# A routed feed-forward layer behind a graph convolution: loading and turning the first slot within the convolution, more row buffers, and slot tables in two steps

## The chip, the cores and the metric

The kernel runs on one core of a Trainium2 chip. A core has five engines that run their own instruction streams in order: TensorE (PE in the profile; its weight loads are listed apart as PEld), VectorE (DVE), ScalarE (ACT), GpSimd (POOL) and SyncE (SP, which here only issues DMAs; SPq in the profile is its DMA queue, POOLq that of GpSimd). Engines wait for each other and for DMAs on semaphores. On-chip memory is SBUF (128 partitions) and PSUM, in which TensorE accumulates. The metric is the device time of one execution in microseconds (us). The kernel before took 2367.03 us, the median of 15 runs (2361.11 to 2371.93).

## The reference

Four layers with residual connections over 3125 nodes of 256 features: a graph attention layer, a dense mixture layer, a graph convolution (GNN) and a routed feed-forward layer (FFN). The change lies in the last two. Cut to these:

```python
# graph convolution, 2 layers, on layer-normed x
x = relu(input @ weight + bias)
for i in range(2):
    h = x @ conv_w[i]
    msg = h[s] * (dinv[s] * dinv[d])[:, None]          # edges and self-loops
    x = relu(segment_sum(msg, d, num_segments=3125) + conv_b[i])
# x_total = x_before + x

# routed FFN on xt = layernorm(x_total)[3125, 256], 8 experts of width 1024
probs = softmax(xt @ Wr + br)
top_p, top_idx = top_k(probs, 2)
weights = top_p / top_p.sum(-1, keepdims=True)
xn = layernorm(xt)
xe = xn[None] * ln_g[:, None] + ln_b[:, None]          # of each expert
h = gelu(einsum('end,edh->enh', xe, W1) + b1)
y = einsum('enh,ehd->end', h, W2) + b2
out = x_total + sum over the two chosen experts of weights * y[expert]
```

## The kernel before

**The build.** The program is written with tiles taken from pools. A pool with n buffers of a name makes the n+1st tile wait until all users of the first are done. The build adds the waits and orders the instructions of each engine itself; within an engine the order is then fixed. So "is issued after" below is the order of the code, and an engine may run a few instructions in another order.

**The second convolution.** The nodes are 25 blocks of 128. `layer(1, ...)` in `graph_convolutions_fast` goes over five groups of `GB` = 5 blocks (b0 = 0, 5, 10, 15, 20). For each group it loads the counts of edges between blocks in five pieces (`cnt_h`, three buffers, by SP), casts each piece (`cnt_r`, two buffers: three fifths on ACT at L1093, two fifths on DVE at L1094), and adds 125 matmuls of 128x128 by 128x512 into five PSUM accumulators `po` (L1099). When a block is summed, DVE scales both halves of `po` (L1112, L1114) and adds to the residual stream (L1173). After the last block of a group, the tasks of `Router.tasks` for this group go into a list `spare`; `layer` calls these between the matmuls of the next group. The tasks of the last group (b0 = 20) are called in the routed slots.

**Routing.** For one group of blocks: layer norm into `rt_xt` (L1030); five `logits` (a block is turned on PE into PSUM `aux` and multiplied with `wr`, L2479); `choose` (softmax and the two best, DVE and ACT); four empty tasks; `place` (two matmuls with a strict lower triangle and with ones count how many rows each expert has had before; DVE makes the row index and the marks weight and node number); a second layer norm; five `send`. A `send` makes two rows per node of 258 numbers, the 256 features copied by ACT (L2551) and the two marks by DVE (L2552), in a tile `rt_row` that has four buffers, and scatters each of the two to the DRAM array `rows` by an indirect DMA of POOL (L2553). `rows` has a range for each expert. Then five `begin` store the blocks of the residual stream to `out` (L2563), to which the slots later add.

**Slots.** The routed layer is computed in slots of 256 rows of one expert (24 full ones, then half ones). Slots 0 to 7 (`SOON` = 8) take rows of blocks below 15 (`KNOWN`) alone, since after group b0 = 10 it is known how many slots those fill. `close(15)`, after the sends of group b0 = 10, makes the table of the expert and first row of these slots (`share_soon`), and `close(25)`, after the sends of the last group, that of all others (`share_late`). Both end with twelve small matmuls against `close_mine` that put each slot's bias and layer norm vectors into columns (L2600 and L2607 in the profile; there as 16 and 8, since each of these float32 matmuls has two records) and two ACT copies. `add_up` (L2630) makes running sums of 8 or 16 columns by as many additions, each of one column to the one before.

For a slot s, `load(s)` reads expert and first row from the table into SP's registers and issues on SP the rows `xr` (L2708, 264 KB), the weights w1 and w2 (L2715 and L2717, 1 MB each) and the bias b2 (L2719). The load of rows waits for the scatters that may hold its rows: for slots below 8 those of blocks below 15, for later ones all. Because they are in one DRAM array, the build also makes any scatter and any load wait for what stands before it, unless they are declared to have nothing to do with each other; the scatters are so among each other (`apart(ins, "rows")`). `front(s)` turns the rows with four PE transposes into PSUM (L2732, tile `tr`), scales them by the slot's vectors into `xe` (DVE, L2735), and makes the output indices `free` (L2741) and `to` (L2743) from the marks. `slot(s)` computes eight pieces `ph` of the hidden layer (L2757) with GELU on ACT (L2759), calls `front` of the next slot, then two `py` (L2767), adds bias and weight on DVE into `y` (L2770, L2771) and adds the rows to `out` by an indirect DMA of POOL (L2772). A full slot has 32 records of ph and 32 of py. After each piece of ph and of py one task is taken from `spare` as long as there are any.

**Where slot 0 stands.** `load(0)` is called after `layer(1, ...)`, from the pool `ahead`. `begin_slots` then calls `load(1)` and `front(0)`, and in a loop over s = 0 to 7 `load(s + 2)` and `slot(s)`. At s = 6 the tasks still in `spare` are called at once, since `load(8)` needs the late table.

Of the kernel before, what the change touches and what calls it, by code (L numbers as in the profile page):

```python
# [11 lines left out]
F32 = mybir.dt.float32  # L12
# [749 lines left out]
class Fast(Kernel):  # L762
# [277 lines left out]
    def graph_convolutions_fast(self, I, router, experts, out):  # L1040
# [5 lines left out]
        with ExitStack() as ctx:  # L1046
# [129 lines left out]
                    spare.extend(router.tasks(b - GB + 1, GB, out))  # L1176
            layer(1, work, finish1)

            router.load(0, I)
            second.close()  # L1180
            router.begin_slots(out, I)

# [1177 lines left out]
class Router:  # L2360
# [15 lines left out]
    def __init__(self, k):  # L2376
        self.k, self.tc, self.nc = k, k.tc, k.nc
        NS, SLOT = self.NS, self.SLOT
        self.rows = k.dram.tile([8 * self.RANGE + SLOT, self.W], F32, name="rows")
        self.scatters, self.spare, self.at = [], deque(), {}  # L2380

    def prepare(self, ctx):
        nc = self.nc
        NS, NF = self.NS, self.NF
        pool = self.pool = ctx.enter_context(self.tc.tile_pool(name="router", bufs=1, reuse_waits="tile"))
        self.more = pool.tile([1, 1], I32, name="more")

        self.parts = [(0, self.SOON), (self.SOON, NS - self.SOON)]
# [32 lines left out]

    def open(self, ctx, aux, I):
        nc = self.nc
        work = ctx.enter_context(self.tc.tile_pool(name="route_work", bufs=1, reuse_waits="tile"))
        self.ahead = ctx.enter_context(self.tc.tile_pool(name="ffn1_ahead", bufs=1, reuse_waits="tile"))
        self.work, self.aux = work, aux
# [29 lines left out]
    def tasks(self, b0, n, out):  # L2456
# [89 lines left out]
        def send(i):  # L2546
            b = b0 + i
            m = min(P, N - b * P)
            for r in range(2):
                row = work.tile([P, self.W], F32, name="rt_row", bufs=4)  # L2550
                nc.scalar.copy(row[:, :D], st["xt"][:, i, :])  # L2551
                nc.vector.tensor_copy(row[:, D:], st["mark"][:, r, i, :])  # L2552
                ins = nc.gpsimd.indirect_dma_start(  # L2553
                    out=self.rows, out_offset=bass.IndirectOffsetOnAxis(
                        ap=st["index"][:m, r, i:i + 1], axis=0),
                    in_=row[:m, :], in_offset=None)
                self.apart(ins, "rows")
                self.scatters.append((b, ins))

        def begin(i):  # L2560
# [3 lines left out]
            if b0 + n == NB:  # L2564
                self.tc.declare_no_dep(ins.ins, group="soon",
                                       reason="the first slots' rows are of earlier blocks")

        each = range(n)
        tasks = ([norm] + [lambda i=i: logits(i) for i in each] + [choose] +
                 [lambda: None] * 4 + [place, renorm] + [lambda i=i: send(i) for i in each])  # L2570
        if b0 + n in (self.KNOWN, NB):
            tasks.append(lambda: self.close(b0 + n))
        return tasks + [lambda i=i: begin(i) for i in each]

    def close(self, blocks):


        nc = self.nc
        late = blocks == NB
        n = self.parts[late][1]  # L2580
        table, b1, ln = self.table[late], self.b1[late], self.ln[late]
        one = lambda shape, name: self.work.tile(shape, F32, name="close_" + name, bufs=1)
        total = one([P, 8], "total")
        nc.vector.tensor_sub(total, self.next[:, blocks, :], self.next[:, 0, :])
# [6 lines left out]
                                op0=ALU.min)  # L2591
        nc.vector.tensor_scalar(owner, owner, 7.0, None, op0=ALU.min)
        nc.vector.tensor_copy(table[:, 0, :], owner[0:1, :])
        mine = one([8, n], f"mine{n}")
        nc.vector.tensor_scalar(mine, owner[:8, :], self.part[:8, :], None, op0=ALU.is_equal)
        rows, F = self.rows8, self.F
        ps = self.pl.tile([P, 512], F32, name="pl")[:, :self.NF * n].rearrange(
            "p (c s) -> p c s", s=n)
# [24 lines left out]
        nc.vector.tensor_reduce(begin, past, AX.X, ALU.add)  # L2623
        nc.vector.tensor_sub(begin, unit, begin)

    def add_up(self, first, need, m):
        nc = self.nc
        nc.vector.memset(first[:, 0:1], 0.0)
        for e in range(m):
            nc.vector.tensor_add(first[:, e + 1:e + 2], first[:, e:e + 1], need[:, e:e + 1])  # L2630

    def share_soon(self, n, total, owner, begin, one):

        nc, SLOT, J = self.nc, self.SLOT, self.SOON
# [7 lines left out]
        self.add_up(first, need, 8)  # L2642
        slot = one([P, n], "slot")
        nc.gpsimd.iota(slot, pattern=[[1, n]], base=0, channel_multiplier=0,
                       allow_small_or_imprecise_dtypes=True)
        self.owners(n, 8, first, slot, need, owner, begin, one)
        nc.vector.tensor_scalar(begin, begin, float(SLOT), None, op0=ALU.mult)
        nc.vector.tensor_scalar(first, first, float(n), None, op0=ALU.min)
        nc.vector.tensor_sub(self.done, first[:, 1:], first[:, :8])

    def share_late(self, n, total, owner, begin, one):
# [20 lines left out]
        self.add_up(first, units, 16)  # L2672
        nc.vector.tensor_add(units, units, at[:, :16])
        nc.vector.tensor_sub(units, units, at[:, 1:])

# [18 lines left out]
    def load(self, s, I):  # L2694
# [12 lines left out]
        xr = pool.tile([P, 2, self.W], F32, name="xr")[:, :self.blocks(s)]  # L2707
        load = nc.sync.dma_start(xr, self.rows[ds(at, self.blocks(s) * P), :].rearrange(  # L2708
            "(i p) w -> p i w", p=P))
        if s < self.SURE:  # L2710
            for b, scatter in self.scatters:
                if late or b < self.KNOWN:
# [9 lines left out]
    def front(self, s):  # L2722
# [1 line left out]
        nc, work = self.nc, self.slot_work  # L2724
        late = s >= self.SOON
        i = s - self.parts[late][0]
        ln, m = self.ln[late], self.blocks(s)
        xr, w1, w2, b2 = self.at.pop(s)
        pt = self.ps_t.tile([P, 2, 2, P], F32, name="tr")
        for c in range(2):  # L2730
            for h in range(m):
                nc.tensor.transpose(pt[:, c, h, :], xr[:, h, c:D:2], self.k.ident)  # L2732
# [3 lines left out]
                                    ln[:, 0, c, i:i + 1], ln[:, 1, c, i:i + 1], op0=ALU.mult,  # L2736
                                    op1=ALU.add)

        to = work.tile([P, 2], I32, name="to", bufs=6)[:, :m]
        free = work.tile([P, 2], F32, name="free", bufs=2)[:, :m]  # L2740
        nc.vector.tensor_scalar(free, xr[:, :, D + 1], 0.0, float(2 * NP), op0=ALU.is_lt,  # L2741
                                op1=ALU.mult)
        nc.vector.tensor_add(to, free, xr[:, :, D + 1])  # L2743
# [37 lines left out]
    def begin_slots(self, out, I):  # L2781
# [5 lines left out]
        with tc.tile_pool(name="ps_h0", bufs=2, space=PSUM, reuse_waits="tile") as self.ps_h, \  # L2787
                tc.tile_pool(name="ps_t0", bufs=1, space=PSUM, reuse_waits="tile") as self.ps_t, \
                tc.tile_pool(name="ps_y0", bufs=2, space=PSUM, reuse_waits="tile") as self.ps_y:
            self.load(1, I)  # L2790
            self.front(0)
            for s in range(self.SOON):
                if s + 2 == self.SOON:
                    while self.spare:
                        self.spare.popleft()()
                self.load(s + 2, I)
                self.slot(s, s + 1, I, out)

# [92 lines left out]
```

## Time and profile before

One execution was profiled; all times below of parts of the kernel are of this one.

| what | value |
|---|---|
| median of 15 runs | 2367.03 us (2361.11 to 2371.93) |
| profiled execution, own time | 2364.63 us |
| its span on the core | 2362.8 us |
| mean granted TensorE clock | 0.945 of full speed |
| PE busy | 2053.6 us (87%) |
| PEld busy | 1712.1 us (72%) |
| DVE busy | 1335.0 us (57%) |
| ACT busy | 1085.7 us (46%) |
| POOL busy | 808.7 us (34%) |

The busy time in 40 slices of 59 us each shows where the engines are full; each digit is a tenth of the slice:

```
PE   5577788888988876899999699979989978999996
DVE  7798576768777763278888443334327664212221
ACT  3498556555666546044544254434434433222231
POOL 1777777777777723000000500000001313221221
PEclk9999999999999888999999799989999988999998
DMA  7545575756767759962221100033325445667773
```

The stretch of this change lies in slices 31 to 34 (counted from 1): the second convolution with its routing from 1750 on, the end of the convolution at 1929.98, slot 0 from 1943.71 and slot 1 from 1963.71. From there on the slots follow each other to the end. PEclk is the clock granted to TensorE in tenths; it is 8 where the others around it are 9. The busy time of a group of instructions in the profile holds its work at a low clock too, so a longer busy time may be the same work. An idle time in the profile is followed by what ended it: "9.07 <-DMA xr<-rows" means that PE stood still for 9.07 us and that the load of xr from rows ended it.

### The profile page before, as it was taken

The page shows a single profiled execution, that of the slowest core. Times are in us where ns is not written, and L with a number is a line of the kernel's source. Part 1 is how long each engine was busy: PE and PEld are TensorE (multiplying, and loading weights), DVE is VectorE, ACT ScalarE, POOL GpSimd, SP SyncE. Part 2 cuts the span into 40 slices and gives each one's busy share as a digit, 9 for nine tenths or more (in the row PEclk, how much of TensorE's full clock was granted, in tenths as well). Part 3 has the DMA queues.
Part 4 walks back from the last instruction along what each step waited for, and adds up shares of the span by engine and source line. Part 5 has one row for each costly group of instructions (what it writes and reads, how often), then busy time and mean ns, then how long its engine had stood idle before and what let it go on. Part 6 is the DMA issues. An engine that isn't in the chain of part 4 may idle for free. (4 is left out here: it accounts for less than half of the span.)

```text
span 2362.8 us, 35957 instructions
## 1 busy us (share of the span) xinstructions
PE 2053.6 (87%) x10512; PEld 1712.1 (72%) x10512; DVE 1335.0 (57%) x4399; ACT 1085.7 (46%) x2496; POOL 808.7 (34%) x801
## 2 busy tenths in 40 slices
PE   5577788888988876899999699979989978999996
PEld 5356677666766655788887588858877767888886
DVE  7798576768777763278888443334327664212221
ACT  3498556555666546044544254434434433222231
POOL 1777777777777723000000500000001313221221
PEclk9999999999999888999999799989999988999998
DMA  7545575756767759962221100033325445667773
GB/s 233 154 122 153 133 209 141 211 168 195 200 190 212 204 159 324 319 209 82 73 70 47 40 1 1 1 111 113 124 100 169 150 135 181 189 190 226 215 215 72
DMA packets 236521, 356.91 MB, mean 151 GB/s; under 512 B 37356, under 2 KB 177923, under 8 KB 232603
## 3 DMA queue, kind: packets, MB, share of 16 engines
q1 hardware_dynamic: 194315, 258.97, 33.9%
q0 software_dynamic: 39008, 92.91, 15.4%
q10 hardware_dynamic: 2992, 2.62, 0.4%
q8 instruction: 88, 1.44, 0.3%
q14 instruction: 118, 0.97, 0.1%
HBM read 268.69 MB, written 86.20 MB: 150 GB/s over the span
## 5 line engine op out<-in xcount | busy, mean ns | idle before, releaser
L1876 POOL DMA_INDIRECT edge_rows<-table,pick x566 | 591.4, 1045 | 184.0 <-issue 74.3
L1961 PE MATMUL edge_sums<-edge_moves,edge_rows 128*128 128x120 f32 x2264 | 332.3, 294 | 76.0 <-DVE agg L1974 74.7
L1961 PEld LDWEIGHTS edge_sums<-edge_moves,edge_rows 128*128 128x128 f32 x2264 | 309.0, 206 | 113.7 <-DVE agg L1974 91.6
L1099 PE MATMUL po<-parts,cnt_r 128*128 128x512 f32 x1250 | 311.0, 404 | 14.6 <-ACT cnt_r L1093 9.4
L1099 PEld LDWEIGHTS po<-parts,cnt_r 128*128 128x128 f32 x1250 | 236.5, 192 | 64.6 <-ACT cnt_r L1093 10.2
L854 PE MATMUL po<-h,w 128*128 128x257 f32 x1250 | 277.0, 382 | 3.5 <-ACT o L1006 2.3
L854 PEld LDWEIGHTS po<-h,w 128*128 128x128 f32 x1250 | 237.2, 191 | 39.0 <-ACT o L1006 3.9
L1764 PE MATMUL ps<-hot_key,hot_lo 128*128 128x350 f16 (+2 forms) x782 | 193.1, 335 | 70.5 <-DVE acc L1790 35.0
L1782 ACT CAST acc<-ps 128x325 f32 (+2 forms) x391 | 179.1, 458 | 140.2 <-PE ps L1764 106.5
L1744 DVE TENSOR_SCALAR hot_key<-iota_key,key 128x350 f16<-128x350 f16 (+2 forms) x782 | 235.4, 330 | 4.4 <-PE ps L1764 3.2
L2759 ACT ACTIVATE hid<-ph,ffn_b 128x256 f32<-128x256 f32 (+1 forms) x232 | 105.8, 456 | 263.5 <-PE ph L2757 261.0
L2757 PE MATMUL ph<-xe,ffn_w 128*128 128x256 f32 (+1 forms) x928 | 194.4, 367 | 3.6 <-DVE rt_xt L1030 3.6
L2772 POOL DMA_INDIRECT out<-y,to x53 | 82.6, 1559 | 317.1 <-DVE y L2771 171.7
L2767 PE MATMUL py<-ffn_w,hid 128*128 128x256 f32 x848 | 189.8, 381 | 1.3 <-ACT hid L2759 1.3
L2757 PEld LDWEIGHTS ph<-xe,ffn_w 128*128 128x128 f32 x928 | 165.1, 194 | 27.0 <-DVE rt_xt L1030 3.9
L2767 PEld LDWEIGHTS py<-ffn_w,hid 128*128 128x128 f32 x848 | 159.3, 191 | 22.0 <-ACT hid L2759 1.7
L839 ACT ACTIVATE z<-z,att_cols 128x640 f32<-128x640 f32 x125 | 103.0, 828 | 146.2 <-DVE z L837 119.9
L1750 ACT ACTIVATE hot_lo<-iota_key,lo 128x128 f16<-128x128 f16 x494 | 170.0, 395 | 0.0
L1764 PEld LDWEIGHTS <-hot_lo 128*128 128x128 f16 x782 | 72.6, 104 | 117.1 <-ACT hot_lo L1757 42.6
L1093 ACT CAST cnt_r<-cnt_h 128x1920 fp32r<-128x1920 f16 x50 | 89.9, 1799 | 112.1 <-PE po L1099 102.9
L2433 POOL IOTA earlier<- 128x128 f32 x1 | 0.2, 243 | 395.0 <-PE po L1099 395.0
L845 DVE TENSOR_TENSOR w<-z,cnt 128x640 f32<-128x640 f32 x125 | 102.4, 820 | 41.3 <-PE po L854 38.4
(422 smaller groups left out, 3253.0 us busy)
## 6 DMA issues: line engine op xcount, KB each, us to landing
ffn_w<-in_L_ffn_W SPq DMA_DIRECT2D x58, 1024.0 KB
cnt_h<-cnt SPq DMA_DIRECT2D x50, 800.0 KB
rows<-blank SPq DMA_DIRECT2D x109, 258.0 KB
cnt<-acc SPq DMA_DIRECT2D x50, 400.0 KB
cnt<-cnt SPq DMA_DIRECT2D x25, 800.0 KB
normed<-first_out SPq DMA_DIRECT2D x20, 640.0 KB
first_out<-first SPq DMA_DIRECT2D x56, 192.0 KB
edge_rows<-table,pick POOLq DMA_INDIRECT x566
```

The costliest lines, as they stand in the source:

```text
L839: nc.scalar.activation(z, z, AF.Exp, bias=cols[:, 0, j:j + 1], scale=-1.0)
L854: nc.tensor.matmul(pos[i][:, :D + 1], lhsT=w[:, ts(i, P)], rhs=moving[:, j, :D + 1], start=(j == 0), stop=(j == NB - 1))
L1099: nc.tensor.matmul(pos[b], lhsT=c[:, j - j0, ts(b, P)], rhs=parts[i][:, j].rearrange("p a m -> p (a m)"), start=(j == 0), stop=(j == NB - 1))
L1744: nc.vector.tensor_scalar(h[:, u, :NB * w], self.wide[:, :NB * w], self.key[:, t:t + 1], None, op0=ALU.is_equal)
L1750: nc.scalar.activation(l[:, u, :], self.wide[:, :P], AF.Abs, bias=self.lo[:, t:t + 1], scale=-1.0)
L1764: last = self.nc.tensor.matmul(ps[:, :n], lhsT=l[:, u, :], rhs=h[:, u, :n], start=(u == 0), stop=(u == CT - 1))
L1782: ins = self.nc.scalar.copy(self.acc[g][:, :, ds(o + 1, width(c) - 1)], self.parts[c][:, :, 1:])
L1876: return self.nc.gpsimd.indirect_dma_start(out=self.ring[:, e % (RB * BT), :], out_offset=None, in_=self.table, in_offset=bass.IndirectOff ...
L1961: nc.tensor.matmul(ps[:, f * 4 * w:f * 4 * w + EW], lhsT=self.rows_of(m)[:, e, ts(f, P)], rhs=self.spread[m % 3][:, e * 5 * w:e * 5 * w + EW],
L2757: nc.tensor.matmul(ph, lhsT=w1[:, c, ts(f, P)], rhs=xe[:, c, :], start=(c == 0), stop=(c == 1))
L2759: nc.scalar.activation(hid[:, f, :], ph, AF.Gelu, bias=b1[:, f:f + 1])
L2767: nc.tensor.matmul(py, lhsT=hid[:, f, ts(i, P)], rhs=w2[:, f, :], start=(f == 0), stop=(f == NF - 1))
```

## The change

- `load(0)` is taken out from behind `layer(1, ...)`. The tasks of group b0 = 10 get it, at the end: `close(0)`, two empty tasks, `close_vectors(0)`, `load(0)`, then the five stores `begin`. That makes 28 tasks in this group instead of 24.
- `front(0)` is taken out of `begin_slots`. In the tasks of group b0 = 15 it takes the place of the third of the four empty tasks behind `choose`. It uses the PSUM tile `aux` instead of `tr`, and xe, to and free come from the pool `ahead` with one buffer.
- The row loads of slots 1 to 7 join the group of the scatters (`apart`): the build then makes none of them wait for a later scatter and no scatter wait for them. Their written dependency on the scatters of blocks below 15 stays. The load of slot 0 is not in the group.
- `rt_row` gets eight buffers instead of four.
- `close` is split in two: the tables, up to `close_mine`, and `close_vectors`, the twelve small matmuls and two copies. The late `close_vectors(1)` is called in slot 6, behind six empty tasks.
- `add_up` makes the running sums by doubling: three steps for 8 columns and four for 16, each a copy of the first columns and one addition of the others, in a new tile for each step but the last.

```diff
@@ graph_convolutions_fast
             layer(1, work, finish1)
 
-            router.load(0, I)
             second.close()
             router.begin_slots(out, I)
@@ Router.tasks, send
-                row = work.tile([P, self.W], F32, name="rt_row", bufs=4)
+                row = work.tile([P, self.W], F32, name="rt_row", bufs=8)
@@ Router.tasks
         each = range(n)
+        wait = lambda: None
+        first = (lambda: self.front(0)) if b0 == self.KNOWN else wait
         tasks = ([norm] + [lambda i=i: logits(i) for i in each] + [choose] +
-                 [lambda: None] * 4 + [place, renorm] + [lambda i=i: send(i) for i in each])
-        if b0 + n in (self.KNOWN, NB):
-            tasks.append(lambda: self.close(b0 + n))
+                 [wait, wait, first, wait] + [place, renorm] + [lambda i=i: send(i) for i in each])
+        if b0 + n == self.KNOWN:
+            tasks += [lambda: self.close(0), wait, wait, lambda: self.close_vectors(0),
+                      lambda: self.load(0, self.I)]
+        elif b0 + n == NB:
+            tasks.append(lambda: self.close(1))
         return tasks + [lambda i=i: begin(i) for i in each]
@@ Router.close
-        mine = one([8, n], f"mine{n}")
+        mine = self.mine[late] = one([8, n], f"mine{n}")
         nc.vector.tensor_scalar(mine, owner[:8, :], self.part[:8, :], None, op0=ALU.is_equal)
+
+    def close_vectors(self, late):
+
+        nc, n, mine = self.nc, self.parts[late][1], self.mine[late]
+        b1, ln = self.b1[late], self.ln[late]
         rows, F = self.rows8, self.F
...
@@ Router.add_up
-    def add_up(self, first, need, m):
-        nc = self.nc
+    def add_up(self, first, need, m, one):
+
+        nc, step = self.nc, 1
         nc.vector.memset(first[:, 0:1], 0.0)
-        for e in range(m):
-            nc.vector.tensor_add(first[:, e + 1:e + 2], first[:, e:e + 1], need[:, e:e + 1])
+        while step < m:
+            out = first[:, 1:] if 2 * step >= m else one([P, m], f"sums{m}_{step}")
+            nc.vector.tensor_copy(out[:, :step], need[:, :step])
+            nc.vector.tensor_add(out[:, step:], need[:, step:], need[:, :m - step])
+            need, step = out, 2 * step
@@ Router.load
+        if 0 < s < self.SOON:
+            self.apart(load, "rows")
         if s < self.SURE:
             for b, scatter in self.scatters:
                 if late or b < self.KNOWN:
@@ Router.front
-        ln, m = self.ln[late], self.blocks(s)
+        ln, m, deep = self.ln[late], self.blocks(s), 1 if s == 0 else 6
         xr, w1, w2, b2 = self.at.pop(s)
-        pt = self.ps_t.tile([P, 2, 2, P], F32, name="tr")
+        if s == 0:
+            work, pt = self.ahead, self.aux.tile([P, 512], F32, name="aux").rearrange(
+                "p (c h n) -> p c h n", c=2, h=2)
+        else:
+            pt = self.ps_t.tile([P, 2, 2, P], F32, name="tr")
...
-        to = work.tile([P, 2], I32, name="to", bufs=6)[:, :m]
-        free = work.tile([P, 2], F32, name="free", bufs=2)[:, :m]
+        to = work.tile([P, 2], I32, name="to", bufs=deep)[:, :m]
+        free = work.tile([P, 2], F32, name="free", bufs=min(deep, 2))[:, :m]
@@ Router.begin_slots
             self.load(1, I)
-            self.front(0)
             for s in range(self.SOON):
                 if s + 2 == self.SOON:
                     while self.spare:
                         self.spare.popleft()()
+                    self.spare.extend([lambda: None] * 6 + [lambda: self.close_vectors(1)])
                 self.load(s + 2, I)
                 self.slot(s, s + 1, I, out)
```

More of the change, by code (lines that the diff above doesn't have):

```diff
@@ L2379, in __init__ @@
         self.rows = k.dram.tile([8 * self.RANGE + SLOT, self.W], F32, name="rows")
-        self.scatters, self.spare, self.at = [], deque(), {}
+        self.scatters, self.spare, self.at, self.mine = [], deque(), {}, {}
     def prepare(self, ctx):
@@ L2386, in prepare @@
         self.more = pool.tile([1, 1], I32, name="more")
+        self.slot_work = None
         self.parts = [(0, self.SOON), (self.SOON, NS - self.SOON)]
@@ L2423, in open @@
         nc = self.nc
+        self.I = I
         work = ctx.enter_context(self.tc.tile_pool(name="route_work", bufs=1, reuse_waits="tile"))
@@ L2568, in tasks, with close @@
         each = range(n)
+        wait = lambda: None
+        first = (lambda: self.front(0)) if b0 == self.KNOWN else wait
         tasks = ([norm] + [lambda i=i: logits(i) for i in each] + [choose] +
-                 [lambda: None] * 4 + [place, renorm] + [lambda i=i: send(i) for i in each])
-        if b0 + n in (self.KNOWN, NB):
-            tasks.append(lambda: self.close(b0 + n))
+                 [wait, wait, first, wait] + [place, renorm] + [lambda i=i: send(i) for i in each])
[4 more added lines that the diff above has]
+            tasks.append(lambda: self.close(1))
         return tasks + [lambda i=i: begin(i) for i in each]
-    def close(self, blocks):
+    def close(self, late):
         nc = self.nc
-        late = blocks == NB
+        blocks = NB if late else self.KNOWN
         n = self.parts[late][1]
-        table, b1, ln = self.table[late], self.b1[late], self.ln[late]
+        table = self.table[late]
         one = lambda shape, name: self.work.tile(shape, F32, name="close_" + name, bufs=1)
@@ L2641, in share_soon @@
         first = one([P, 9], "first")
-        self.add_up(first, need, 8)
+        self.add_up(first, need, 8, one)
         slot = one([P, n], "slot")
@@ L2671, in share_late @@
         first = one([P, 17], "first_unit")
-        self.add_up(first, units, 16)
+        self.add_up(first, units, 16, one)
         nc.vector.tensor_add(units, units, at[:, :16])
```

## The prediction

> **What bounds the kernel now.** I read the engine table first: TensorE (PE) is busy 87% of a span of 2362.8 us, and nearly full in the last sixth. The change touches only the stretch from about 1800 to 2010 us: the second convolution's five groups, then the first three routed slots. There I read the waits of PE, then the busy time by stretch, then the lines around each gap.
>
> Waits of PE between 1800 and 2010 us (total, times, longest):
>
> ```profile
> engine line waited for: us in total, times, longest us
> PE tr L2732 <- DMA xr<-rows: 9.1, 1, 9.1
> PE pl L2600 <- DVE close_mine L2595: 5.4, 1, 5.4
> PE po L1099 <- DVE o L1114: 4.8, 2, 2.6
> PE ph L2757 <- DVE rt_xt L1030: 3.6, 1, 3.6
> PE pl L2600 <- issue: 2.2, 1, 2.2
> PE py L2767 <- ACT hid L2759: 1.3, 1, 1.3
> PE po L1099 <- DVE cnt_r L1094: 0.4, 1, 0.4
> ```
>
> These are 26.8 us of idle PE. The cost does not end with them: after most gaps the granted clock is about half. Busy time by stretch (PE, weight loads, DVE, ACT, POOL, then clock, DMA share, GB/s):
>
> ```profile
> 1885.00:1895.00 10.00, 10.00 (x32) 8.11 (x33) 3.51 (x11) 3.13 (x7) 5.46 (x6) 0.54 0.53 168
> 1944.00:1949.00 5.00, 5.00 (x15) 3.98 (x15) 2.67 (x13) 1.65 (x4) 0.00 (x0) 0.51 0.98 317
> 1949.00:1964.00 15.00, 15.00 (x86) 13.40 (x85) 7.88 (x29) 10.40 (x19) 0.25 (x1) 1.00 1.06 376
> 1985.00:1997.00 12.00, 12.00 (x40) 10.14 (x41) 1.11 (x4) 1.51 (x4) 4.50 (x3) 0.51 0.31 59
> 2012.00:2340.00 328.00, 328.00 (x1635) 290.59 (x1634) 67.23 (x190) 91.58 (x202) 70.67 (x46) 1.00 0.68 197
> ```
>
> PE is "full" at 0.51 to 0.54, doing half the work. Following the granted clock finely, the half-clock stretches are 1853.33 to 1856.74 (3.41), 1884.05 to 1894.29 (10.24), 1935.25 to 1948.90 and 1983.03 to 1996.69 (13.65 each). A stretch costs half of the part of it in which PE works. From 2012 on PE never waits, so what is saved before slot 2 is saved at the end.
>
> Where the gaps come from, from the timeline (start, length, instruction, idle before it and its releaser):
>
> ```profile
> 1853.25 8.00 PE L1099 MATMUL po<-parts,cnt_r 128*128 128x512 f32 x27 [2.61 <-DVE o L1114]
> 1932.86 0.96 POOL L2553 DMA_INDIRECT rows<-rt_row,rt_index  x1 [0.30 <-issue]
> 1936.10 0.41 SPq L2708 DMA_DIRECT2D xr<-rows  x1
> 1939.05 1.10 PE L2732 MATMUL tr<-ident,xr 128*128 128x128 f32 x4 [9.07 <-DMA xr<-rows]
> 1943.71 3.75 PE L2757 MATMUL ph<-xe,ffn_w 128*128 128x256 f32 x8 [3.56 <-DVE rt_xt L1030]
> 1984.92 3.58 PE L2600 MATMUL pl<-close_mine,rows 8*128 8x24 f32 x16 [5.39 <-DVE close_mine L2595]
> ```
>
> The reader should see a chain: the last of group 15's ten scatters starts at 1932.86; SP issues slot 0's row load 3.2 us later, when that has landed; the rows land at 1939.05; PE waits 9.07 us. And what DVE and ACT wait for in the same window:
>
> ```profile
> DVE rt_row L2552 <- DMA rows<-rt_row,rt_index: 30.2, 23, 3.8
> ACT rt_row L2551 <- DMA rows<-rt_row,rt_index: 36.9, 20, 5.0
> ```
>
> With four row buffers, the fifth to tenth row of each group wait for a scatter on an in-order engine, ahead of the sums that would free PE's accumulators.
>
> **The change part by part.** Times are on the axis of the profiled execution: span 2362.8, own time 2364.6, which is 2.4 under the median of the runs.
>
> *Eight row buffers.* A scatter lands 2.8 to 3.9 us after it starts, and POOL starts one per 1.27. Before, DVE is held until the sixth has landed (3.9 + 5 x 1.27 = 10.2 us from the first start), now until the second (5.2). It comes free 5 us earlier, more than either gap behind "o" (2.14 and 2.61, at 1814 and 1850). Both go, and with them the half-clock stretch behind the second (3.41 / 2 = 1.7): 6.4. Late next are the casts: four more row copies stand ahead of one on ACT, some 1.4 us by the row copies' 0.41 and the overlap of their starts, against some 1.75 of slack by my reading of the two orders. A bound from below is 4 (one stretch and one gap stay).
>
> *Slot tables of group 10.* PE's 2.22 gap before the small matmuls is a wait for the DVE chain. In the changed order these matmuls stand two convolution matmuls earlier (22 of the last 30 ahead instead of 24), and the chain is still behind the ninth row's wait. So I leave 2.0 of the gap. Whether the 10.24 of half clock recurs I can't read: 0 to 5.1 gained. I take half, 2.6: the gap before is unchanged in kind, but less idle time precedes it. Slot 0's four transposes move into the layer at 0.64 (full clock, from slot 1's row). Sum 0.2 + 2.6 - 0.6 = 2.2, ends -0.4 to 4.7.
>
> *Slot 0 loaded and turned early.* Its row load needs only blocks below 15, whose last scatter started at 1894.08, so it can land near 1900. Group 15's scatters (from 1921.48) now wait for it, with 21 us to spare. On SP the load (rows, 2 x 1 MB of weights, bias) goes ahead of five output stores and the 25th count load, which also waits for the lane of the first weight load. That count load is needed near 1915 and should be there by 1905: nothing. On DVE the "free" operation on slot 0's rows stands ahead of a cast; by my reading of the order it has 1.6 to 3.3 us of slack: nothing, but every us beyond is a us of PE. The first bias operations, xe (1.0 us on DVE) in group 15, lie beside PE.
>
> From the layer's end (1929.98) to slot 1's first matmul (1963.71) it took 33.7: 13.7 of waits and transposes, then slot 0's 20.0. Now slot 0's ph starts at once. The 20.0 holds 5.2 at half clock, 2.6 lost: 17.4 without. New is a wait in the middle: PE reaches slot 1's transposes after 12 ph matmuls (0.28 each, four took 1.11 at 1950.18: 3.3), but slot 1's row load is behind the stores of blocks 20 to 23 on SP, and these wait for DVE's last sums. On DVE five blocks take 1.12 each after the tenth row; the stores take 1.08 each to issue (two took 2.17 on SP). That puts the load some 4.3 after the layer's end, and rows land 2.95 after issue (1936.10 to 1939.05): 7.2, a wait of 3.9 and some 0.2 of restart, 4.1. It is long enough for a half-clock stretch; I take two of the short ones, 2 x 1.7 = 3.4, between 0 and 6.8. New: 17.4 + 4.1 + 3.4 = 24.9. Gain 8.8, ends 5.4 (stretch as long as the one now) and 12.2 (none).
>
> *Vectors of the late slots to slot 6.* From slot 1's first ph (1963.71) to slot 2's transposes (2001.44): 37.7. Steady slots take 14.3. Out go the 5.39 gap, the vector matmuls 3.58 + 1.90 = 5.5 at half clock, and half clock over the rest of that stretch (11.8 busy, less 5.5, by half: 3.1). 37.7 - 5.4 - 5.5 - 3.1 = 23.7; ACT's 1.30 gap stays; with 0.5 for place's matmul group, no longer behind a wait, 23.2. The 24 small matmuls come back in slot 6, 2.7 at full clock, 5.5 at half; I take 3.3. Gain 14.5 - 3.3 = 11.2, ends 5.8 (the 5.39 comes back as a wait of slot 2 for DVE) and 12.
>
> *Doubling.* 8 serial additions become 6 operations, 16 become 8. By the row "close_first_unit" six took 1.12 us, 0.19 each: 0.4 and 1.5 us less on DVE, with the copies off the chain. No PE work waits there any more except the small matmuls of group 10: nothing by itself.
>
> *Early loads free of later scatters.* Loads 1 to 7 lose a wait that only load 0 (30.4 us on SP's queue) showed large. Already priced above.
>
> Sum: 6.4 + 2.2 + 8.8 + 11.2 = 28.6. Profiled 2364.6 - 28.6 = 2336; against the median, 2338.
>
> [...]
>
> **The rivals.**
> 1. *Clock stays low at every gap that is left.* For it: gaps of 2.2 and 2.6 were each followed by it. Against: the gap of 2.14 at 1814 was not. Then 2.6 (tables) + 3.4 (slot 1's wait) + 2.2 (slot 6) less gain: 2338 + 8 = 2346.
> 2. *New waits take the place of the old.* Slot 2's xe, in DVE's order, stands behind the late tables' chain, and slot 1's rows come later still. Gives back 5.4 and, with a longer store queue, 4 and a further stretch of 5: 2338 + 14 = 2352. For it: DVE showed 30.2 us of row waits. Against: four more buffers remove most.
> 3. *Short gaps cost no clock.* 2.6 + 3.4 + 0.6 more: 2331.
> 4. *Slower.* Load 0 holds SP's queue: it waits for every scatter lane, and the 25th count load stands behind its weights. PE then starves in group 20. To lose 28.6 and 4.7 more, the count load would have to land 33 us after it is needed, near 1948 instead of 1905, or slot 0's rows be 35 us late at DVE. Scatters of group 10 all started by 1894.08, which speaks against it.
> 5. *It doesn't do what it says.* Load 0 lands late enough that slot 0 has to wait as before, and only the buffers gain: 2367 - 6 = 2361.
>
> **How the numbers follow.** Forecast 0.47, rival 1 0.22, rival 2 0.12, rival 3 0.09, rival 5 0.04, slower 0.06. Low: rival 3's 2331 less the upper ends of the buffers and slot 6, about 4: 2327. High: rival 2 with 2, 2354; above lie rivals 4 and 5. A measurement here tells 0.2% (4.7 us) from no change: faster 0.91, same 0.03, slower 0.06.
>
> **What would show it.** The wait of "tr" for xr falls from 9.1 to about 4 and names slot 1; "pl <- close_mine" 5.4 is gone, the 2.2 stays; "po <- o" 4.8 is gone; DVE's row waits fall from 23 times to about 8; clock near 1.00 through slots 1 and 2; PE continuous from about 1957 on. Wrong if PE shows waits for cnt_r in the last group (load 0 in the way), if slot 2's ph waits for xe, or if slot 6 shows a new gap.

## The result and the profile after

The changed kernel takes 2336.78 us, the median of six runs (2334.06 to 2340.68); the kernel before took 2366.96 in the runs beside it (31 runs). The ratio is 0.9876, 95% interval 0.9863 to 0.9890, so it is faster by 1.24%, 30 us. The forecast was 2338. The profiled execution took 2332.42, its span 2330.6.

The waits of PE between 1800 and 2010 us of the changed kernel (total, times, longest):

```profile
PE pl L2611 <- issue: 2.0, 1, 2.0
PE tr L2753 <- DMA xr<-rows: 1.5, 1, 1.5
PE ph L2778 <- DVE o L1114: 0.9, 1, 0.9
PE aux L1037 <- DVE rt_xt L1030: 0.6, 1, 0.6
```

Five us of waits stand where there were 26.8. The 9.1 for slot 0's rows, the 3.6 behind it, the 5.4 for "close_mine" and both gaps behind "o" are gone; the 2.2 ahead of the early small matmuls is still there as 2.0. New are 1.5 for slot 1's rows, 0.9 for the last sum of the convolution ("o") and 0.6 for a layer norm ("rt_xt"). DVE's and ACT's waits for scatters, same window:

```profile
ACT rt_row L2552 <- DMA rows<-rt_row,rt_index: 27.2, 9, 5.5
DVE rt_row L2553 <- DMA rows<-rt_row,rt_index: 18.9, 9, 4.6
```

They are fewer (9 instead of 23 on DVE), and each is longer. Busy time by stretch (PE, PEld, DVE, ACT, POOL, clock, DMA share, GB/s):

```profile
1874.00:1884.00 10.00, 10.00 (x30) 8.04 (x30) 3.61 (x7) 2.16 (x3) 6.19 (x7) 0.50 0.53 174
1928.00:1963.00 35.00, 35.00 (x182) 30.50 (x181) 21.81 (x114) 19.98 (x41) 11.64 (x11) 1.00 0.71 231
2010.00:2024.00 14.00, 14.00 (x76) 11.85 (x75) 1.89 (x6) 3.96 (x10) 3.45 (x3) 1.00 0.71 199
2024.20:2027.50 3.30, 3.30 (x10) 2.68 (x9) 0.99 (x2) 0.19 (x1) 1.08 (x1) 0.50 0.47 77
```

The half clock of group 15 is back in full length (1873.95 to 1884.19, again 10.24 us). Behind the convolution's end the clock stays at 1.00, where two stretches of 13.65 stood. A short new one follows the late small matmuls in slot 6, though PE was busy through the whole stretch before it.

From the times of PE's matmuls the two executions part as follows (us). The third column is the kernel before once more, from a later run told below.

| stretch | before | before, again | changed |
|---|---|---|---|
| up to the second convolution's first matmul | 1750.0 | 1756.3 | 1746.9 |
| its five groups | 30.1, 33.0, 36.2, 47.6, 33.0 | 31.0, 33.0, 36.1, 48.0, 33.0 | 30.3, 33.2, 33.4, 43.0, 33.6 |
| convolution | 179.96 | 181.10 | 173.48 |
| from its end to slot 3's transposes | 71.46 | 71.50 | 42.82 |
| from there to PE's end | 343.36 | 343.36 | 348.43 |
| after PE's end | 17.96 | 17.86 | 19.06 |

The last four rows give 6.5 + 28.6 - 5.1 - 1.1 = 28.9 us. The other 3.2 us between the two spans lie ahead of anything the change touches, and two executions of the same kernel differ there by 6.

### The profile page after: what moved, and what is told of

Read it like the earlier page. It is cut to its first block, busy times and chain, and to the rows that moved or that the text cites. A ratio compares the mean times of both kernels' runs of the same rounds, so it can differ in the third digit from the quotient of the medians.

```text
span 2330.6 us, 35927 instructions
## 1 busy us (share of the span) xinstructions
PE 2040.0 (88%) x10512; PEld 1699.9 (73%) x10512; DVE 1331.8 (57%) x4389; ACT 1085.9 (47%) x2497; POOL 805.9 (35%) x801
## 5 line engine op out<-in xcount | busy, mean ns | idle before, releaser
L1763 PE MATMUL ps<-hot_key,hot_lo 128*128 128x350 f16 (+2 forms) x782 | 192.6, 335 | 70.9 <-DVE acc L1789 33.4
```

The lines of the kernel that those rows point to most:

```text
L1763: last = self.nc.tensor.matmul(ps[:, :n], lhsT=l[:, u, :], rhs=h[:, u, :n], start=(u == 0), stop=(u == CT - 1))
```

## The experiments

Twelve runs follow, on chips of two kinds. On the chip of the last four everything is as in the profiles above. On the two chips of the first eight the kernel before takes 2498 and 2509 us; some 130 to 150 us more pass ahead of the second convolution, and single instructions there wait for something that the profile calls "remote", an event that nothing in this core's trace accounts for. No profile of the first kind has such a wait. So runs are compared within a kind, and the first comparison is that of the changed kernel itself. On the second kind two limits hold. The changed kernel ran on the chip with 2509, but the runs with four buffers, slot 0 late, the vectors at once and the buffers alone on the one with 2498. And a profile is one execution: those of slot 0 late and of the buffers alone are 6.7 and 7.8 us faster than the medians of their own runs. So a few us between two profiles there show a mechanism better than a price.

**The changed kernel on the second kind of chip.**

> The changed kernel once more, as the measure for the other runs of its chip: the ratio to the kernel before was 0.988. On the chip of the first four runs everything before the convolution took some 130 us longer and single instructions showed waits of 2 to 10 us for something outside the core. If that is the chip's doing, the changed kernel on the same chip is at 2470 to 2480, with slot 1's rows late by some 7 us after the convolution, as in the runs with four buffers and with vectors at once; on a chip like the first it is at 2334 to 2341.

It took 2496.1 us against 2509.14, ratio 0.9951 (0.9932 to 0.9971): 13 us, not 30; it lies 16 us above the range that was expected here. The convolution takes 175.76 us, the stretch to slot 3's transposes 54.79 instead of 42.82. PE's and ACT's waits from 2076 to 2131 us, the first two slots:

```profile
PE ph L2778 <- ACT hid L2780: 4.7, 2, 3.2
PE ph L2778 <- issue: 4.3, 1, 4.3
ACT hid L2780 <- remote: 12.9, 3, 8.8
```

The wait of 4.3 is in slot 0, where the same kernel waits 0.9 on the first chip, and the timeline has around it:

```profile
2079.89 0.48 DVE L1114 SCALAR_TENSOR_TENSOR o<-po,dinv,o 128x256 f32<-128x256 f32 x1
2080.51 3.75 PE L2778 MATMUL ph<-xe,ffn_w 128*128 128x256 f32 x8 [4.35 <-issue]
2081.34 0.47 ACT L2780 ACTIVATE hid<-ph,ffn_b 128x256 f32<-128x256 f32 x1 [8.75 <-remote]
```

PE goes on right behind DVE's last sum "o", the releaser that the profile of the first chip names at this place. DVE had stood 2.4 and 0.9 us among its last sums, the second time for something remote; what held it the first time stays open. Slot 0's first gelu stood 8.75 us on ACT for something remote, but it began only after PE had gone on, so it did not hold PE. Later a gelu did: one that stood 3.8 us for something remote ended the wait of 3.2. PE lost 9.4 us in all instead of 3.0, and had two stretches of 6.83 at half clock. 6.4 us of idle and some 5 of half clock make most of the 12.

**Four row buffers again; slot 0 late again; the vectors at once.** These undo one part each.

```diff
-                row = work.tile([P, self.W], F32, name="rt_row", bufs=8)
+                row = work.tile([P, self.W], F32, name="rt_row", bufs=4)
```

> The changed kernel with four row buffers again. By the sum: the gaps behind "o" return and the convolution takes 6 to 7.5 us longer than the 173.5 of the changed kernel: 2342 to 2345. Rival: the rows also hold DVE in slots 0 and 1, ahead of xe and of the sums of the last blocks, and the stretch from the convolution's end to slot 3's transposes (42.8 in the changed kernel) grows by 5 or more: 2348 to 2352.

Ratio 0.9956 (0.9933 to 0.9980), not to be told from the 0.9951 of the changed kernel on a like chip. The convolution took 178.22 us, 2.5 longer. A gap of 1.79 us behind "o" returned in the third group, and one of 2.06 at the old place in the fourth, which the profile puts down to "remote". But the wait for the early tables fell from 2.37 to 0.30. Neither 6 to 7.5 nor the rival's 5 in the slots (53.66 there) came.

```diff
             layer(1, work, finish1)
 
+            router.load(0, I)
             second.close()
...
-        first = (lambda: self.front(0)) if b0 == self.KNOWN else wait
+        first = wait
...
             tasks += [lambda: self.close(0), wait, wait, lambda: self.close_vectors(0),
-                      lambda: self.load(0, self.I)]
+                      wait]
...
             self.load(1, I)
+            self.front(0)
```

> The changed kernel with slot 0 loaded and turned after the convolution, as before; all else as changed. By the sum the 9.1 and 3.6 us of waits return with the half clock behind them: from the convolution's end to slot 3's transposes 54 to 58 us instead of 42.8, less 0.6 in the convolution: 2347 to 2352. Rival: with the rows sent earlier (eight buffers) the last scatter lands earlier, and only 5 to 6 us of wait return: 2342 to 2345.

Ratio 0.9977 (0.9959 to 0.9995); the stretch behind the convolution is 61.39 us, 6.6 longer than the changed kernel's. Waits of the old length are back, 2050 to 2125 us:

```profile
PE aux L2754 <- DMA xr<-rows: 9.1, 1, 9.1
PE ph L2779 <- DMA ffn_w<-in_L_ffn_W: 3.5, 1, 3.5
PE ph L2779 <- ACT hid L2781: 3.2, 2, 2.4
```

12.6 us return, and a half-clock stretch of 13.65. That is more than the 6.6: the changed kernel's own wait of 4.3 in slot 0 and its stretch of 6.83 there are missing with slot 0 late. So the part is worth 6 to 7 us on this kind of chip by the profiles and the medians, though the intervals of the two ratios overlap. The 9.1 is the load's, as in the prediction and as long as on the first chip; the 3.5 is named for the weights here, not for "rt_xt".

```diff
-            tasks.append(lambda: self.close(1))
+            tasks += [lambda: self.close(1), lambda: self.close_vectors(1)]
...
-                    self.spare.extend([lambda: None] * 6 + [lambda: self.close_vectors(1)])
```

> The changed kernel with the late vectors straight behind the late tables, as before, instead of in slot 6. If the wait for close_mine is what was saved (11.2 us in the sum), it returns with its half clock: 2343 to 2349, and PE shows a wait of 2 to 5 us for close_mine in slot 1 or 2. Rival: with eight buffers and the shorter chain the tables are ready in time anyhow; then nothing is lost, slot 6 loses its 5 us, and the time is 2335 to 2338.

Ratio 0.9941 (0.9918 to 0.9963), not told from the changed kernel. PE's waits, 2052 to 2130 us:

```profile
PE ph L2778 <- DVE o L1114: 5.6, 1, 5.6
PE pl L2611 <- issue: 2.8, 1, 2.8
PE pl L2618 <- ACT ffn_b L2612: 2.6, 1, 2.6
```

The 5.4 for the tables has become 2.8, and the 2.6 comes of a copy on ACT that waited 9.7 for something remote. The stretch to slot 3 takes 60.21 us, 5.4 more, and the slots from there 343.40, 3.4 less, since slot 6 is free of the small matmuls. So here moving the vectors gains 2 us of the 11.2 that the prediction put there. The signs that were expected did come, a wait of 2.8 ahead of slot 2 with 10.24 us of half clock behind it; PE went on at 2105.28, right behind DVE's close_mine (2105.14), though the profile names "issue". What is missing is the time. But the changed kernel has losses of its own in the same two slots on this kind of chip, the 4.7 for gelus and 6.83 at half clock. From slot 1's first ph to slot 3's transposes (us):

| kernel | us |
|---|---|
| before, first kind | 37.5 |
| eight buffers alone, second kind | 34.3 |
| changed with the vectors at once, second kind | 34.8 |
| changed, second kind | 30.7 |
| changed, first kind | 22.6 |

The buffers alone have no remote wait in these slots, the vectors at once the one of 2.6. Against the 22.6 that makes 10 to 12 us, less the 5 that slot 6 takes more on the first kind: 5 to 7. That is an estimate; the vectors at once were not run on a chip of the first kind.

**Eight row buffers alone, in the kernel before.**

```diff
-                row = work.tile([P, self.W], F32, name="rt_row", bufs=4)
+                row = work.tile([P, self.W], F32, name="rt_row", bufs=8)
```

> The kernel before with eight row buffers and nothing else. If the two gaps behind "o" and the half-clock stretch behind the second came from rows waiting for scatters, they go: the five groups of the convolution take 173 to 174 us instead of 180.0 (first to last L1099 matmul), the time is 2359 to 2361. Rival: each gap only moves to the next wait on DVE (the ninth row), and the convolution takes 178 or more, 2365 to 2367. A side effect that neither term has in it: the late table's chain on DVE stands behind fewer row waits, so PE's wait for close_mine of 5.4 us in slot 2 may shrink to about 1 and its stretch of half clock with it, another 4 to 8 us (2352 to 2356).

Ratio 0.9983 (0.9967 to 0.9999): 4 us, less than expected. The convolution takes 175.19, 1 to 2 more than expected, the third group 33.7 (36.2 in the profile of before on the first kind) and the fourth 44.0 (47.6); both gaps are gone. The side effect came in part. PE's waits, 2050 to 2125 us:

```profile
PE tr L2732 <- DMA xr<-rows: 8.4, 1, 8.4
PE pl L2600 <- DVE table L2590: 3.7, 1, 3.7
PE ph L2757 <- DVE ng_mv L1025: 2.2, 1, 2.2
```

The 5.4 for the tables is 3.7 with the buffers alone, not 1, and the stretch of half clock behind it 10.24 instead of 13.65; from the convolution's end to slot 3's transposes it takes 66.30 us.

**Serial sums.** The function of before in the changed kernel.

```diff
-        while step < m:
-            out = first[:, 1:] if 2 * step >= m else one([P, m], f"sums{m}_{step}")
-            nc.vector.tensor_copy(out[:, :step], need[:, :step])
-            nc.vector.tensor_add(out[:, step:], need[:, step:], need[:, :m - step])
-            need, step = out, 2 * step
+        for e in range(m):
+            nc.vector.tensor_add(first[:, e + 1:e + 2], first[:, e:e + 1], need[:, e:e + 1])
```

> The changed kernel with the serial running sums. By the sum they lie beside other work: within 2 us of the changed kernel, the wait of 2.0 us for the early tables longer by at most 0.5. Rival: the chain for the early tables is on the path and the wait grows by 1 or more, since other DVE work interleaves with every link of a longer chain.

Ratio 0.9935 (0.9910 to 0.9960) against 0.9951; the wait ahead of the early small matmuls is 2.48 us against 2.37. The doubling gains nothing that shows.

**The vectors dealt out.** The twelve small matmuls as tasks of their own; the early ones in the next group.

```diff
-            tasks += [lambda: self.close(0), wait, wait, lambda: self.close_vectors(0),
-                      lambda: self.load(0, self.I)]
+            tasks += [lambda: self.close(0), lambda: self.load(0, self.I)]
...
+        heads = [norm] + [lambda i=i: logits(i) for i in each]
+        if b0 == self.KNOWN:
+            v = self.vector_tasks(0)
+            heads = [t for h, task in enumerate(heads) for t in [task] + v[2 * h:2 * h + 2]]
...
-                    self.spare.extend([lambda: None] * 6 + [lambda: self.close_vectors(1)])
+                    self.spare.extend(self.vector_tasks(1))
```

> The changed kernel, but the small matmuls of the vectors are dealt out among other matmuls: the late twelve one per task in slots 6 and 7, the early ones in the tasks of the next group of blocks, where the tables are long ready; slot 0's load follows the early tables at once. If the small matmuls in a row and PE's wait ahead of them are what brings the clock down, both stretches go: 10.24 us in the fourth group (5.1 us of work) and 3.41 behind slot 6 (1.7), with the 2.0 us of wait: 8 to 9 us less than the changed kernel. Rival: the half-clock stretch of the fourth group comes of the whole routing work there (transposes, logits, small matmuls together) and recurs: 2 to 4 us less.

Ratio 0.9980 (0.9958 to 1.0002), median 2502.92 us: 7 us more than the changed kernel on the same chip, not 8 to 9 less, though the intervals overlap. The fourth group is as expected, 35.35 us instead of 44.19, gap and half clock gone. But the last group takes 46.26 instead of 33.72. The timeline there:

```profile
2035.94 0.40 SPq L2754 DMA_DIRECT2D xr<-rows  x1
2038.67 0.17 DVE L2793 TENSOR_SCALAR free<-xr 128x2 f32<-128x2 f32 x1 [5.22 <-DMA xr<-rows]
2040.41 1.12 PE L1037 MATMUL aux<-ident,rt_xt 128*128 128x128 f32 x4 [3.13 <-DVE rt_xt L1030]
```

This is the prediction's fourth rival at small size. Slot 0's rows leave on SP when POOL's scatters have landed, at 2035.94 here, 3.2 us after the last began, and 3.9 after it in the changed kernel on this chip; PE being 9 us ahead, DVE stands 5.2 us at "free", the norm and a cast wait behind it, PE waits 3.1 and then has 10.24 us of half clock. In the changed kernel on this chip the load left at 2041.27 and DVE came to "free" at 2045.63 without a wait: 1.4 us of slack, if the rows take the 2.95 us of before to land. On the first chip it is 3 (1884.78 and 1890.78). In slots 6 and 7, dealing the late ones out costs more than doing them in a row: from slot 6's transposes to slot 7's and on to slot 8's it takes 18.43 and 16.50 us, against 17.64 and 14.32 in the changed kernel on the same chip.

**All 128 rows.** The vectors' matmuls over 128 rows, the others zero.

```diff
-        rows = self.rows8 = one([8, self.F + 2 * D], "rows8")
+        rows = self.rows8 = one([P, self.F + 2 * D], "rows8")
+        nc.vector.memset(rows, 0.0)
...
-        mine = self.mine[late] = one([8, n], f"mine{n}")
-        nc.vector.tensor_scalar(mine, owner[:8, :], self.part[:8, :], None, op0=ALU.is_equal)
+        mine = self.mine[late] = one([P, n], f"mine{n}")
+        nc.vector.tensor_scalar(mine, owner, self.part, None, op0=ALU.is_equal)
```

> The changed kernel with the vectors' matmuls over 128 rows instead of 8, the others zero (the same sums). In slot 6 PE had no gap and yet the clock fell right behind the 24 records. If it falls because only 8 of 128 rows are used, it stays at 1.00 there now (1.7 us less); if because in these records loading weights and not multiplying takes the time, nothing changes (within 1 us of the changed kernel).

Ratio 0.9946 (0.9930 to 0.9961), no change. The clock fell in slot 6 all the same:

```profile
2180.00:2186.70 6.70, 6.70 (x44) 5.84 (x42) 0.33 (x2) 2.69 (x6) 1.56 (x1) 1.00 0.98 319
2186.80:2190.10 3.30, 3.30 (x11) 2.66 (x12) 0.99 (x2) 0.71 (x2) 0.00 (x0) 0.50 0.64 165
```

PE had no gap, and all rows were in use. So it is not the eight rows. In other runs with the same order in slot 6 it did not fall (below).

**Three mends, on a chip like the first.** Beside them the kernel before was profiled again.

> The kernel before, profiled beside the others. On the two later chips the changed kernel gained 0.5%, not 1.2%. If what is lost there is lost between the convolution's end and slot 3's transposes (42.8 us on the first chip, 54.8 on the later one), the kernel before takes 66 to 70 us for that stretch here and 180 for the convolution, so that only 11 to 16 of 28.6 us are left of that gain. Rival: the stretch takes the kernel before as much longer as the changed one (83), and the gain went elsewhere, before the convolution. If the chip is like the first, its times are those of the first profile.

The chip was like the first: ratio 1.0005 (0.9991 to 1.0020), the stages in the table above. So how the kernel before spends its stretch on the second kind of chip was not seen, and where the other 17 us of the gain went there is settled for the changed kernel's side alone.

The first mend puts the last stores behind slot 1's row load on SP, by order:

```diff
             if b0 + n == NB:
+                self.tc.add_manual_dep(ins.ins, self.first_load.name, ORDER)
                 self.tc.declare_no_dep(ins.ins, group="soon",
...
             self.apart(load, "rows")
+        if s == 1:
+            self.first_load = load.ins
```

> The changed kernel with the stores of the last five blocks behind slot 1's row load on SP, by order alone. If the stores are what makes slot 1's rows late (the wait of 4.1 in the sum), PE's waits between the end of the convolution and slot 1's transposes fall from 4.3 (later chips) or 3.0 (first chip) to 1 or less, and a half-clock stretch of 6.8 with them: 3 to 6 us less than the changed kernel on a later chip, 1 to 3 on one like the first. Rival: slot 1's rows wait for the convolution's buffers, not the stores, or the first gelu on ACT holds PE: within 1 us.

Ratio 0.9876 (0.9855 to 0.9897), the same as the changed kernel. The wait for slot 1's rows is gone. PE's waits, 1800 to 2060 us:

```profile
PE pl L2612 <- issue: 1.8, 1, 1.8
PE ph L2781 <- DVE o L1114: 1.0, 1, 1.0
PE aux L1037 <- DVE rt_xt L1030: 0.8, 2, 0.6
```

So the stores did make the rows late, by 1.5 us. The stretch takes 41.91 instead of 42.82; that is too little for the times to show.

The second has the early vectors in the next group, with the tasks shown above, the late ones in a row, and "free" behind xe by order:

```diff
+        if s == 0:
+            self.tc.add_manual_dep(ins.ins, scaled.ins.name, ORDER)
```

> The changed kernel with the early vectors in the tasks of the next group, as in the run with both dealt out (there the fourth group took 35.4 instead of 44.2 us), the late ones in a row in slot 6 as in the changed kernel, and on DVE the operation "free" on slot 0's rows put behind xe by order alone. If that operation is what held DVE for 5.2 us and PE for 3.1 in the last group, with 10.2 at half clock behind it, the last group is back to 34 to 37 us with the fourth at 35: 6 to 9 us less than the changed kernel. Rival: the wait moves to PE's transposes or the clock falls all the same: the last group takes 42 or more and nothing is won.

Ratio 0.9874 (0.9855 to 0.9894), not told apart either. The fourth group takes 33.0 us instead of 43.0, and the clock is 1.00 through it and the last group, of which this is the most:

```profile
1883.00:1917.00 34.00, 34.00 (x175) 27.66 (x176) 23.14 (x97) 14.80 (x26) 8.71 (x9) 1.00 0.49 170
```

The last takes 37.4 instead of 33.6, with no gap of PE: it has the small matmuls now. DVE comes to "free" without a wait. That the order did this is likely but not shown by itself, since the early vectors did not run without it on this kind of chip. The convolution is 5.3 us shorter. 2.2 of that are lost behind it (44.98 instead of 42.82): slot 1's rows, which hang on the stores, are waited for 2.5 us instead of 1.5, and a stretch of 3.41 at half clock follows.

> The two before this one together. By the sum of both: 9 to 14 us less than the changed kernel on a later chip (2482 to 2487 where that took 2496), 8 to 11 on one like the first (2326 to 2329). Rival: what the first wins is given back, since the convolution ends sooner and slot 0's or slot 1's rows are then later against it: 3 to 6 us less.

Both together: 2334.89 us, ratio 0.9857 (0.9835 to 0.9878). From the convolution's first matmul to PE's end it takes 559.7 us, against 564.7 of the changed kernel, 562.5 and 561.6 of the two mends. That is 5 us, in the rival's range and not 8 to 11, but not for the rival's reason, for what the second mend lost behind the convolution comes back: no wait for slot 1's rows is left, and the stretch takes 41.57 instead of 44.98. Each mend was worth less than forecast: of the 2.2 us of the first, 1.7 are the half clock behind slot 6's small matmuls, which did not come in that run, and here the last group (38.95) has 3.41 us of half clock. By the times alone the 0.9857 is not told apart from 0.9876.

## Why the prediction was right

The sum was 28.6 us and the touched stretches give 28.9. That it came out so close is luck, since errors of up to 4.6 us cancel; step by step:

- **Eight row buffers, 6.4.** Third group 2.9 shorter; in the fourth the gap of 2.61 and the half clock behind it, 1.7, are gone: 7.2. The mechanism stands: alone, the buffers shorten the third group as much (33.7). But taken back on the second kind of chip they cost 2.5 us of convolution, since on the way the wait for the early tables falls. The size was right in the sum; as a price of its own it was not. (In the profile of before scatters land 2.4 to 3.9 us after they start, not 2.8 to 3.9; the step uses the 3.9.)
- **Tables of group 10, 2.2.** The gap kept 2.0, as written. The half clock recurred in full, 10.24 us at 0.50, so the 2.6 taken from the middle of its range was 0. With the transposes this step lost 0.4.
- **Slot 0 early, 8.8.** From the convolution's end to slot 1's first ph (1940.59, among the last py of slot 0): 20.3 instead of the 24.9 expected, a gain of 13.4. The waits were 3.0 instead of 4.1, and only 1.5 of them for slot 1's rows; the 3.4 of half clock did not come (1.00 from 1928 to 1963). Slot 0 undone returned the 9.1 of the row wait.
- **Vectors to slot 6, 14.5 before slot 6.** From slot 1's first ph on: 22.6 instead of 23.2. (The prediction calls 2001.44 slot 2's transposes; they are slot 3's, and the 37.7 us hold about a slot and a half. Slot 1's first ph begins at 1963.92; 1963.71 is the last py of slot 0. The differences are hardly touched by it.) The total is right, but the move does not earn all of it. Eight buffers by themselves bring 37.5 to 34.3, with a wait for the tables of 3.7 instead of 5.4: DVE gets to the tables earlier. With the vectors at once the wait is 2.8, with half clock behind it: the prediction's mechanism at half its size. What the move by itself is worth on the first kind of chip stays open; 5 to 7 of the 11.2 is the estimate above.
- **Slot 6, 3.3.** Slot 6 took 17.64 us against 14.31 steady, 3.3. Behind it came a stretch of 3.41 at half clock, 1.7 more.
- **Doubling and the early loads' waits, nothing.** Serial sums cost nothing that shows. The early loads' missing waits were not tried by themselves.
- **After PE's end, 1.1 more.** Not in the sum; no run was made for it.

Of the rivals, the clock's (1 and 3) each came in part: it was 0.50 behind the gap of 2.0 at the early tables and fell to 0.50 in slot 6, and it was 1.00 behind the waits of 0.9, 1.5 and 0.6 in slot 0. That short gaps cost no clock, as rival 3 has it, was the author's assumption; no run varied the length of a gap alone. The fourth did not come in this kernel, but dealing the vectors out showed its mechanism, and how little slack "free" had.

## What to carry to other kernels

Undo each part before giving it a price: parts that shorten one in-order queue cover for each other (the buffers, 6.4 in the sum, cost 2.5 us of convolution when taken back, as another wait fell from 2.37 to 0.30), so the prices of a sum that is right need not be. An operation that waits for a load should not stand ahead of other work on its engine, even if it has slack today: making PE 9 us faster took that slack of 1.4 us on one chip, where DVE then stood 5.2, and with one order dependency the wait did not come on another. And compare changes on one chip: the same change was worth 30 us on one and 13 on another.

## What was new about the hardware

The clock of TensorE fell without a gap. In slot 6, 24 records of 128x24 float32 in 3.1 us, PE busy throughout (14.00 of the 14 us from 2010 on), were followed by a half-clock stretch in the changed kernel (0.50 from 2024.20 to 2027.50) and in three other runs, one of them that with all 128 rows (0.50 from 2186.80 to 2190.10); in a fifth (four row buffers) it began among them. In four more with the same small matmuls in a row none came, one of them the changed kernel on the second kind of chip (1.00 from 2183 to 2190). In the changed kernel on the first:

```profile
2019.62 1.96 PE L2611 MATMUL pl<-close_mine,rows 8*128 8x24 f32 x16
2022.14 1.12 PE L2618 MATMUL pl<-close_mine,rows 8*128 8x24 f32 x8
2024.23 8.72 PE L2788 MATMUL py<-ffn_w,hid 128*128 128x256 f32 x32
```

The 32 py records take 7.07 us at full clock and 8.72 here. The half-clock stretches told of here are 3.41, 6.83, 10.24 and 13.65 us long, one to four times 3.41. In the kernel before one of 3.41 (1853.33 to 1856.74) came behind a gap of 2.61 us, and the clock was 1.00 from 1810 to 1820, around a gap of 2.14; here no gap stood ahead of it. Why it comes in some runs and not in others was not shown.

On the second kind of chip single ACT instructions stood up to 9.7 us for "remote" events in the first slots and up to 10.2 earlier on. In the changed kernel there the "acc" casts of ACT lost 45 us in sum to them and "agg" of DVE 44. What they are stays open.
